# A dense 3x3 convolution of 192 channels on TensorE: 96 + 96 channels in 18 passes, or 128 + 64 channels in 15 passes with two image halves side by side

## The chip, the core and the metric

The kernel runs on one core of one Trainium2 chip. The time is device microseconds of that core for one execution of the whole kernel, and the median of several executions is given. TensorE is called PE below, the weight loads of TensorE PEld, VectorE DVE, ScalarE ACT, GpSimd POOL, and SyncE SP (its queue issues the transfers). All numbers are float32.

## The reference, cut to what matters

Four layers work on x of 16 images, 192 channels and 32 x 32 pixels, each with a residual and a group norm ahead of it. Only layer 0 is concerned here. After an mLSTM block over the 1024 pixels of an image (layer norm, projections, a scan that the kernel does in chunks of 128 pixels, an output projection) it has this end:

```python
y = x1 + x2                      # mLSTM block + silu(seq @ w_lin + b_lin)
y = conv_general_dilated(y, conv2_w, (1, 1), ((1, 1), (1, 1)), ("NCHW", "OIHW", "NCHW"))
y = y + conv2_b[None, :, None, None]
mu = y.mean((0, 2, 3)); var = y.var((0, 2, 3))        # over all 16 images
y = (y - mu) / sqrt(var + 1e-5) * bn_g + bn_b
x = x + where(y >= 0, y, 0.01 * y)
```

So 192 channels go to 192 channels with nine taps, 16 times 1024 pixels, and layer 1 can't begin before the mean and variance over all images are known.

## The kernel before, in words

layer0 goes through 128 chunks of 128 pixels, eight for an image, four for a unit (half an image, 512 pixels). The loop over g (layer0_step) does the work of one chunk: p = scores x decays on DVE (L680), num and state on PE (L694, L706, L729), the scores of the next chunk (L649), the normalisation (layer0_norm) and the output of the chunk before (layer0_output). Beside it run "side" tasks, each a generator with a start and a due time in steps: Side.tick lets each advance in proportion to the time gone by. The front of a unit (layer0_front: load of x, group norm and layer norm, w_up at L502, w_lin at L522, w_q and w_k at L540) has 2.7 steps, twice an image. The convolution of an image (layer0_conv2) has the time from 9.2 steps after the image's first chunk on, four parts of 1.9 steps each.

What an engine then does in which order is settled when the program is built: a scheduler goes through the instructions by priority and by when their operands should be there, and fixes one order for each engine. Each engine works off its own order strictly, and waits where an operand isn't there. [...]

layer0_down (L782 on) writes half of an image into ypad: 96 partitions, 2 halves of the channels, and the image of 32 x 32 with a frame of zeros, 34 x 34. There are two ypad tiles, for even and odd images. layer0_conv2 reads ypad directly, with shifted views for the nine taps. A part is 96 outputs of half an image (16 rows, 512 pixels): nine taps times two halves of the input channels make 18 matmuls of 96 rows, 96 columns and 512 pixels that add up in one PSUM tile, "conv", of which there is one. Four parts are 72 matmuls an image. In the trace each f32 matmul is two records. Then ACT adds the bias (L465), DVE takes the statistics (L466), and a transfer stores y to y0 in DRAM (L467). After the last chunk the four parts of the last image are done with nothing beside them, and batch_norm (L312 on) makes scale and shift from the statistics. Layer 1 (layer1_front) loads y0 again.

Other matmuls already put several outputs on different columns of TensorE: depthwise (L1094), in layers 2 and 3, gives three or four outputs of 32 channels, ps[32 * g : 32 * g + 32].

Of the kernel before, what the change touches and what calls it, by code (L numbers as in the profile page):

```python
# [10 lines left out]
F32 = mybir.dt.float32  # L11
# [7 lines left out]
C = 192  # L19
HP = 96  # L20
DI = 384
S = 1024
W = 32
# [73 lines left out]
def lay_out(a):  # L97

    p96, p128 = Pack(HP), Pack(128)
    for n in ("ln_w", "ln_b", "b_down", "b_lin", "conv2_b", "bn_g", "bn_b"):  # L100
        p96.vec("0" + n, a["L0_conv_" + n])
    for n in ("b_up", "conv_k", "conv_b", "skip", "mh_w", "mh_b"):
        p128.vec("0" + n, a["L0_conv_" + n])
    gates = np.zeros((128, 2), np.float32)
    gates[:NH, 0] = a["L0_conv_b_i"]
    gates[:NH, 1] = a["L0_conv_b_f"]
    p128.add("0gates", gates)
    for n in ("norm_w", "norm_b", "proj_b"):
        p96.vec("1" + n, a["L1_conv_" + n])
    p96.add("1skip_scale", np.broadcast_to(a["L1_conv_skip_scale"].reshape(1, 1), (HP, 1)))  # L110
    p128.add("1conv_r", taps(a["L1_conv_conv_w"].reshape(DI, 1, 4)))
    for n in ("conv_b", "A_log", "D"):
        p128.vec("1" + n, a["L1_conv_" + n])
    p96.add("2w_r", taps(a["L2_conv_w"].reshape(C, 3, 3)))
    for n in ("b", "gamma", "beta"):
        p96.vec("2" + n, a["L2_conv_" + n])
    for n in ("b_out", "dw_b", "bn_g", "bn_b", "bn_mean", "bn_var", "pw_b"):
        p96.vec("3" + n, a["L3_conv_" + n])
    p96.add("3dw_r", taps(a["L3_conv_dw_w"].reshape(C, 3, 3)))
    p96.vec("3r_w", a["L3_conv_r_w"].T)  # L120
    p96.add("3r_b", np.broadcast_to(a["L3_conv_r_b"].reshape(1, 2), (HP, 2)))
    p128.add("3conv_r", taps(a["L3_conv_conv_w"].reshape(DI, 4, 4)))
    for n in ("b_in", "conv_b", "ln_g", "ln_b"):
        p128.vec("3" + n, a["L3_conv_" + n])
    p128.vec("3Ds", a["L3_conv_Ds"].T)
    p128.vec("3A_log", a["L3_conv_A_log"].transpose(1, 0, 2))

    def in96(w):
        return w.reshape(2, HP, -1).transpose(1, 0, 2)

    def in128(w):
        return w.reshape(w.shape[0] // 128, 128, -1).transpose(1, 0, 2)

    def dt_rows(w, b):
        o = np.zeros((64, DI), np.float32)
        o[:RK], o[XD] = w.T, b
        return o

    def pair(f, *v):
        rows = [np.concatenate([f(*(x[k] for x in v)), f(*(x[k + 2] for x in v))]) for k in range(2)]  # L140
        return np.stack(rows, 1)[: 64 + XD + 1]

    def x_rows(w):
        return np.concatenate([w, np.zeros((64 - XD, DI), np.float32)])

    wif = np.zeros((3 * DI, 44), np.float32)
    wif[:, :NH] = a["L0_conv_w_i"]
    wif[:, 32 : 32 + NH] = a["L0_conv_w_f"]
    const, const0 = shape_constants()
    arrays = {  # L150
        "x": a["x"].reshape(-1, C, S),
        "p96": p96.array(),
        "p128": p128.array(),
        "const": const.array(),
        "const0": const0.array(),
        "w0_up": in96(a["L0_conv_w_up"]),
        "w0_q": in128(a["L0_conv_w_q"]),
        "w0_k": in128(a["L0_conv_w_k"]),
        "w0_qt": in128(a["L0_conv_w_q"].T),
        "w0_kt": in128(a["L0_conv_w_k"].T),  # L160
        "w0_if": in128(wif),
        "w0_down": in128(a["L0_conv_w_down"]),
        "w0_lin": in96(a["L0_conv_w_lin"]),
        "w0_conv2": in96(a["L0_conv_conv2_w"].transpose(1, 2, 3, 0).reshape(C, 9 * C)),
        "w1_in": in96(a["L1_conv_in_proj_w"].T),
        "w1_x": in128(x_rows(a["L1_conv_x_proj_w"])[: XD + 1].T),
        "w1_dt": dt_rows(a["L1_conv_dt_proj_w"], a["L1_conv_dt_proj_b"])[: XD + 1],
        "w1_out": in128(a["L1_conv_out_proj_w"].T),
        "w1_proj": in96(a["L1_conv_proj_w"].T),
        "w3_in": in96(a["L3_conv_W_in"]),  # L170
        "w3_x": in128(pair(x_rows, a["L3_conv_x_proj_w"]).transpose(2, 1, 0).reshape(DI, -1)),
        "w3_dt": pair(dt_rows, a["L3_conv_dt_proj_w"], a["L3_conv_dt_proj_b"]).reshape(-1, 2 * DI),
        "w3_out": in128(a["L3_conv_W_out"]),
        "w3_pw": in96(a["L3_conv_pw_w"].T),
    }
    arrays = {k: np.ascontiguousarray(v) for k, v in arrays.items()}
    return arrays, p96.at, p128.at, const.at, const0.at
# [74 lines left out]
class Program:  # L252
# [35 lines left out]
    def run(self):  # L288
        tc, nc = self.tc, self.nc
        with tc.tile_pool(name="const", bufs=1) as cp, tc.tile_pool(name="scratch", bufs=1, space=DRAM) as dp:  # L290
            self.p96 = self.load(cp, "p96", list(self.ins["p96"].shape))
            self.p128 = self.load(cp, "p128", list(self.ins["p128"].shape))
            self.const = self.load(cp, "const", list(self.ins["const"].shape))
            self.y0 = dp.tile([self.nb, HP, 2, S], F32, name="y0")
            self.x2 = dp.tile([self.nb, HP, 2, S], F32, name="x2")
            self.y2 = dp.tile([self.nb, HP, 2, S], F32, name="y2")
            self.x3 = dp.tile([self.nb, HP, 2, S], F32, name="x3d")
            self.x1 = dp.tile([self.nb, HP, 2, S], F32, name="x1d")
            self.xf1 = dp.tile([self.nb, HP, 2, S], F32, name="xf1d")
            self.sz3 = dp.tile([2, 2, 128, 3, 512], F32, name="sz3")  # L300
            self.bn0 = cp.tile([HP, 2, 2], F32, name="bn0")
            self.bn2 = cp.tile([HP, 2, 2], F32, name="bn2")
            self.layer0()
            self.layer12()
            self.layer3()
# [64 lines left out]
    def layer0(self):  # L370
        tc = self.tc
        with (
# [5 lines left out]
        ):  # L378
            self.layer0_weights(wp, bp, psum)
            self.stats = wp.tile([HP, 2, 2 * self.nb, 6], F32, name="stats")  # L380
            self.unit, self.image = {}, {}
            n = self.nb * S // 128
            side = Side()
            for i in range(1, self.nb * S // U):
                side.add("front", self.layer0_front(i, sp, bp, dp, psum), NCH * i - 3.9, NCH * i - 1.2)
            for b in range(self.nb - 1):
                for j in range(4):
                    at = 8 * b + 9.2 + 1.9 * j
                    side.add("conv", self.layer0_conv2(b, j, bp, psum), at, at + 1.9)
            finish(self.layer0_front(0, sp, bp, dp, psum))  # L390
            self.layer0_decays(self.unit[0], sp, psum)
            chunks = {0: Chunk(self.unit[0], 0, 0)}
# [3 lines left out]
                for j, _ in enumerate(self.layer0_step(g, n, chunks, sp, bp, psum)):  # L396
                    side.tick(g + j / 8)
            side.close()
            for u in range(4):
                finish(self.layer0_conv2(self.nb - 1, u, bp, psum))  # L400
            self.batch_norm(sp, "0bn_g", "0bn_b", self.bn0)

    def layer0_weights(self, wp, bp, psum):
# [8 lines left out]
        self.w_c2 = self.load(wp, "w0_conv2", [HP, 2, 9, C])  # L412

        self.b_up = wp.tile([128, 6], F32, name="b_up")
        ps = psum.tile([128, 512], F32, name="mm")
# [15 lines left out]
        for c in range(3):  # L431
# [8 lines left out]
        self.v1, self.ypad = [], []  # L440
        for i in range(2):
            v1 = wp.tile([128, NH, DH + 1], F32, name=f"v1{i}")
            nc.vector.memset(v1, 1.0)
            yp = wp.tile([HP, 2, W + 2, W + 2], F32, name=f"ypad{i}")
            nc.gpsimd.memset(yp, 0.0)
            self.v1.append(v1)
            self.ypad.append(yp)

    def layer0_conv2(self, b, part, bp, psum):

        nc = self.nc
        yp = self.ypad[b % 2]
        m, i = divmod(part, 2)
        ps = psum.tile([128, 512], F32, name="conv", bufs=1)
        for t in range(9):
            for k in range(2):
                r0 = 16 * i + t // 3
                nc.tensor.matmul(  # L458
                    ps[:HP], self.w_c2[:, k, t, m * HP : (m + 1) * HP],
                    yp[:, k, r0 : r0 + 16, t % 3 : t % 3 + W],  # L460
                    start=t + k == 0, stop=t + k == 9,
                )
            yield
        y = bp.tile([HP, 512], F32, name="y", bufs=1)
        nc.scalar.activation(y, ps[:HP], AF.Identity, bias=self.v96("0conv2_b", m))  # L465
        nc.vector.bn_stats(self.stats[:, m, 2 * b + i], y)  # L466
        nc.sync.dma_start(self.y0[b, :, m, i * 512 : (i + 1) * 512], y)  # L467

    def layer0_front(self, i, sp, bp, dp, psum):

# [311 lines left out]
    def layer0_down(self, unit, psum):  # L782

        nc = self.nc
        b, u = divmod(unit["i"], S // U)
        yp = self.ypad[b % 2]
        rows = U // W
        for m in range(2):
            ps = psum.tile([128, 512], F32, name="mm")
# [355 lines left out]
    def layer1_front(self, b, sp, bp, psum):  # L1145
# [5 lines left out]
        nc.sync.dma_start(xf, self.y0[b])  # L1151
        yield Wait(1)
        for m in range(2):
            for h in halves():
# [479 lines left out]
```

## Time and profile before

| what | us |
|---|---|
| median of 3 runs | 17707.09 |
| lowest, highest | 17689.62, 17722.61 |
| the profiled execution's own time | 17751.62 |
| its span, first to last instruction | 17749.8 |
| last eviction of the convolution (L465) starts | 4200.95 |

The page gives, for each engine, its busy time in the span; then the span in 40 equal slices of 444 us, where a digit is the busy share in tenths and PEclk is the clock that TensorE was granted, in tenths of full speed. Groups of instructions stand in rows: line, engine, operation, output and inputs, shape, number of records, then busy time and mean duration in ns, then the idle time of the engine ahead of them and what ended it. In answers by window the columns are the stretch, its length, then for each engine busy time and number of records, then the granted clock (1 is full), the DMA share and GB/s. A row of the timeline has the start, the length, engine, line, operation, and in brackets how long the engine had been idle and what ended that. Layer 0 fills the first nine and a half slices.

### The profile page before, as it was taken

Reading aid. Unit: us, or ns where it says so; the run is one execution under the profiler, and the core shown is the slowest. Engines: PE = TensorE matmul, PEld = TensorE weight load, DVE = VectorE, ACT = ScalarE, POOL = GpSimd, SP = SyncE. Lnnn points to the kernel's source line nnn. Section 1 sums busy time; section 2 is a strip of 40 time slices with the busy share of each in tenths; the row PEclk is TensorE's granted clock in tenths of the full one; section 3 lists DMA queues with packets and bytes.
Section 4 is the critical chain, followed back from the end, with each engine's and each line's share of the span. In section 5 each row is a group of like instructions: output and inputs, shape, how many; then the busy total and the mean of one; then the engine's idle time right before and its main releaser. Section 6 shows DMA issues by size and latency. Waiting matters only on the chain. (4 is left out here: it accounts for less than half of the span.)

```text
span 17749.8 us, 263742 instructions
## 1 busy us (share of the span) xinstructions
PE 16096.1 (91%) x99836; PEld 11228.6 (63%) x99836; DVE 13328.7 (75%) x14875; ACT 11899.2 (67%) x19653; POOL 11473.1 (65%) x5556
## 2 busy tenths in 40 slices
PE   8998898898998999988999999999999999999998
PEld 4444444444655555555777777777777777777777
DVE  4454444444777777766898888888888888888888
ACT  2222222223666666656888888888888888888888
POOL 3333333333555555545887888788878888888888
PEclk8898988898999999999999999999999999999999
DMA  1111111112343333333333333333323332333232
GB/s 43 32 31 32 32 31 30 33 30 70 107 116 114 116 118 117 115 102 105 97 108 94 94 99 107 92 96 100 107 85 95 107 105 85 99 106 99 90 98 67
DMA packets 877952, 1511.10 MB, mean 85 GB/s; under 512 B 80337, under 2 KB 311198, under 8 KB 865835
## 3 DMA queue, kind: packets, MB, share of 16 engines
q1 hardware_dynamic: 876682, 1494.22, 28.9%
q8 instruction: 791, 12.96, 0.3%
q14 instruction: 479, 3.92, 0.1%
HBM read 1264.99 MB, written 228.92 MB: 84 GB/s over the span
## 5 line engine op out<-in xcount | busy, mean ns | idle before, releaser
L940 POOL TENSOR_TENSOR h<-h,cb 128x1536 f32<-128x1536 f32 x2560 | 8875.0, 3470 | 1429.5 <-DVE h L933 883.9
L909 ACT ACTIVATE da<-dt,neg_a 128x512 f32<-128x512 f32 x7680 | 5266.5, 714 | 1737.1 <-DVE h L933 1668.3
L933 DVE TENSOR_TENSOR_SCAN h<-da,carry,xb 128x512 f32<-128x512 f32 x3840 | 4652.8, 1262 | 664.4 <-PE xb L920 599.4
L951 PE MATMUL y<-const,h 128*128 128x128 f32 x30720 | 4717.6, 276 | 129.2 <-DVE ysum L1391 54.1
L933 DVE TENSOR_TENSOR_SCAN h<-da,xb 128x512 f32<-128x512 f32 x3840 | 4440.5, 1202 | 387.5 <-PE xb L920 275.3
L917 PE MATMUL xb<-const,xbt 128*128 128x128 f32 x23040 | 4076.6, 282 | 419.3 <-DVE h L933 263.2
L889 ACT ACTIVATE xbt<-ut,bt 128x384 f32<-128x384 f32 x7680 | 4173.9, 603 | 247.3 <-PE xb L917 245.2
L917 PEld LDWEIGHTS xb<-const,xbt 128*128 128x128 f32 x23040 | 2761.4, 143 | 1807.6 <-issue 642.0
L951 PEld LDWEIGHTS y<-const,h 128*128 128x128 f32 x30720 | 3685.1, 143 | 322.4 <-issue 265.3
L920 PE MATMUL xb<-diag,ut 128*128 128x128 f32 x15360 | 3017.2, 279 | 0.0
L920 PEld LDWEIGHTS xb<-diag,ut 128*128 128x128 f32 x15360 | 2384.6, 195 | 62.6 <-issue 62.6
L458 PE MATMUL conv<-ypad,w_conv 96*96 96x512 f32 x2304 | 1258.7, 667 | 3.1 <-ACT y L465 3.1
L899 POOL TENSOR_TENSOR diag<-const,bt 128x512 f32<-128x512 f32 x640 | 681.3, 1065 | 549.6 <-PE xb L920 365.7
L939 POOL COPY carry<-h 128x3 f32<-128x3 f32 x1280 | 250.5, 196 | 1214.2 <-DVE h L933 964.7
L753 POOL TENSOR_TENSOR hs<-h,mhm 128x384 f32<-128x384 f32 x128 | 106.6, 833 | 1023.2 <-DVE den L758 894.5
L636 POOL TENSOR_TENSOR e<-e,const 128x1536 f32<-128x1536 f32 x128 | 444.3, 3471 | 436.5 <-DMA e<-row 380.1
L458 PEld LDWEIGHTS conv<-ypad,w_conv 96*96 96x96 f32 x2304 | 381.4, 181 | 451.2 <-issue 432.1
L839 PE MATMUL mm<-dbl,w_dt 45*128 45x512 f32 x960 | 534.6, 641 | 33.9 <-DVE v L1413 16.2
L638 ACT ACTIVATE e<-e 128x1536 f32<-128x1536 f32 x128 | 189.6, 1481 | 460.6 <-POOL e L637 415.0
L706 PEld LDWEIGHTS num<-v,p 128*128 128x128 f32 x3072 | 427.7, 216 | 78.3 <-issue 56.2
L1094 PE MATMUL mm<-rep,t_dw 96*32 96x512 f32 x2304 | 434.7, 614 | 22.6 <-DMA rep<-xr 16.3
L843 DVE SCALAR_TENSOR_TENSOR dt<-lnsq,mm 128x512 f32<-128x512 f32 x480 | 321.9, 671 | 172.0 <-ACT lnsq L842 172.0
(269 smaller groups left out, 17699.4 us busy)
## 6 DMA issues: line engine op xcount, KB each, us to landing
cb<-row SPq DMA_DIRECT2D x2560, 256.0 KB
rep<-xr SPq DMA_DIRECT2D x384, 331.0 KB
e<-row SPq DMA_DIRECT2D x128, 768.0 KB
rep<-xin SPq DMA_DIRECT2D x384, 256.0 KB
rep<-xr SPq DMA_DIRECT2D x384, 228.8 KB
x<-x SPq DMA_DIRECT2D x48, 768.0 KB
xr<-xin SPq DMA_DIRECT2D x48, 612.5 KB
xr<-xpad SPq DMA_DIRECT2D x32, 867.0 KB
```

The costliest lines, as they stand in the source:

```text
L458: nc.tensor.matmul(ps[:HP], self.w_c2[:, k, t, m * HP : (m + 1) * HP], yp[:, k, r0 : r0 + 16, t % 3 : t % 3 + W], start=t + k == 0, stop=t ...
L636: nc.gpsimd.tensor_tensor(e, e, self.k0("mask")[:, None, :].to_broadcast([128, NH, 128]), ADD)
L839: nc.tensor.matmul(ps, w_dt[:, t * 128 : (t + 1) * 128], dbl, start=True, stop=True)
L889: nc.scalar.activation(t[:, c], u.ut[:, c], AF.Copy, scale=u.bt[:, c, n : n + 1])
L899: nc.gpsimd.tensor_tensor(d, ident[:, None, :].to_broadcast([128, 4, 128]), u.bt[:, 3, n : n + 4][:, :, None].to_broadcast([128, 4, 128]), ...
L909: nc.scalar.activation(da[i, t], u.dt[:, t], AF.Exp, scale=u.neg_a(t, n))
L917: in_order(nc.tensor.transpose(xb[i, t][:, c * 128 : (c + 1) * 128], xbt[i][:, c, t * 128 : (t + 1) * 128], ident))
L920: in_order(nc.tensor.matmul(xb[i, t][:, 384:], u.ut[:, 3, t * 128 : (t + 1) * 128], u.diag[n // 4][:, n % 4], start=True, stop=True, skip_ ...
L933: nc.vector.tensor_tensor_scan(hv, dv, xv, 0.0 if first else u.carry_in[:, n, t : t + 1], MUL, ADD)
L940: nc.gpsimd.tensor_tensor(h[i], h[i], u.c.pop(n)[:, None, :].to_broadcast([128, 3, 512]), MUL)
L951: in_order(nc.tensor.matmul(u.y[:, j], h[i][:, t, c * 128 : (c + 1) * 128], ident, is_transpose=True, start=n == 0 and j % 4 == 0, stop=n ...
L1094: self.nc.tensor.matmul(ps[32 * g : 32 * g + 32], blocks[:, g * side + r], seen, start=r == 0, stop=r == side - 1, skip_group_check=True,)
```

## The change

The input channels are no longer split into 96 + 96 but into 128 + 64, and so are the outputs.

- After layer0_down has filled ypad for an image, layer0_spread writes it to DRAM (yrows) and reads it back in another layout: ya has channels 0 to 127 on 128 partitions; yb has channels 128 to 191 on partitions 0 to 63, and on partitions 64 to 127 the same channels moved by one pixel. These are four transfers on SP's queue, the second to fourth after the first has landed.
- With ya the nine taps take nine passes of 128 rows. With yb two neighbouring taps of the last 64 channels take one pass (three passes of 128 rows), and the third tap of each image row one of 64 rows (three passes). 15 passes in all, not 18.
- Parts 0 and 1 are outputs 0 to 127 for each half of the image: 15 matmuls each. Part 2 is outputs 128 to 191 for both halves: one PSUM tile, the upper half image on columns 0 to 63 and the lower on columns 64 to 127, 30 matmuls in 15 pairs. 60 matmuls an image in three parts of 2.4 steps each.
- There is one ypad, one ya and one yb, for all images. The weights are laid out anew on the host (128 x 15 x 192), y0 is stored by channel, and layer 1 reads it back with a rearranged view.
- The statistics stand by 128 + 64 channels; at the end three stores and a load bring them through DRAM into the old layout, ahead of both batch norms.

The diff, cut to its core:

```diff
             for b in range(self.nb - 1):
-                for j in range(4):
-                    at = 8 * b + 9.2 + 1.9 * j
-                    side.add("conv", self.layer0_conv2(b, j, bp, psum), at, at + 1.9)
+                side.add("spread", self.layer0_spread(b, wp, dp), 8 * b + 9, 8 * b + 9.1)
+                for j in range(3):
+                    at = 8 * b + 9.6 + 2.4 * j
+                    side.add("conv", self.layer0_conv2(b, j, bp, psum), at, at + 2.4)
...
-            for u in range(4):
-                finish(self.layer0_conv2(self.nb - 1, u, bp, psum))
+            finish(self.layer0_spread(self.nb - 1, wp, dp))
+            for j in range(3):
+                finish(self.layer0_conv2(self.nb - 1, j, bp, psum))
+
+            rows = dp.tile([C, self.nb, 2, 6], F32, name="stat_rows", bufs=1)
+            nc = self.nc
+            nc.sync.dma_start(rows[:128], self.stats_a)
+            for i in range(2):
+                nc.sync.dma_start(rows[128:, :, i], self.stats_b[64 * i : 64 * i + 64])
+            nc.sync.dma_start(
+                self.stats, rows.rearrange("(m p) b i s -> p m (b i) s", p=HP)
+            )
...
+    def layer0_spread(self, b, wp, dp):
+        nc = self.nc
+        n = (W + 2) ** 2
+        rows = dp.tile([2, HP, n], F32, name="yrows", bufs=2)
+        nc.sync.dma_start(rows.rearrange("m p t -> p m t"), self.ypad.rearrange("p m a b -> p m (a b)"))
+        rows = rows.rearrange("m p t -> (m p) t")
+        nc.sync.dma_start(self.ya.rearrange("p a b -> p (a b)"), rows[:128])
+        yb = self.yb.rearrange("p a b -> p (a b)")
+        nc.sync.dma_start(yb[:64], rows[128:])
+        nc.sync.dma_start(yb[64:, : n - 1], rows[128:, 1:])
+        yield
...
     def layer0_conv2(self, b, part, bp, psum):
         nc = self.nc
-        yp = self.ypad[b % 2]
-        m, i = divmod(part, 2)
         ps = psum.tile([128, 512], F32, name="conv", bufs=1)
-        for t in range(9):
-            for k in range(2):
-                r0 = 16 * i + t // 3
+        outs = [(ps, 0, 0, part)] if part < 2 else [(ps[64 * i : 64 * i + 64], 128, 128, i) for i in range(2)]
+        for t in range(15):
+            for o, _, c0, i in outs:
+                if t < 9:
+                    src, k, dy, dx = self.ya, 128, t // 3, t % 3
+                else:
+                    src, k, dy, dx = self.yb, 128 if t < 12 else 64, t % 3, 0 if t < 12 else 2
+                r0 = 16 * i + dy
                 nc.tensor.matmul(
-                    ps[:HP], self.w_c2[:, k, t, m * HP : (m + 1) * HP],
-                    yp[:, k, r0 : r0 + 16, t % 3 : t % 3 + W],
-                    start=t + k == 0, stop=t + k == 9,
+                    o, self.w_c2[:k, t, c0 : c0 + o.shape[0]], src[:k, r0 : r0 + 16, dx : dx + W],
+                    start=t == 0, stop=t == 14, skip_group_check=True,
                 )
             yield
```

More of the change, by code (lines that the diff above doesn't have):

```diff
@@ L99, in lay_out @@
     p96, p128 = Pack(HP), Pack(128)
-    for n in ("ln_w", "ln_b", "b_down", "b_lin", "conv2_b", "bn_g", "bn_b"):
+    for n in ("ln_w", "ln_b", "b_down", "b_lin", "bn_g", "bn_b"):
         p96.vec("0" + n, a["L0_conv_" + n])
@@ L103, in lay_out @@
         p128.vec("0" + n, a["L0_conv_" + n])
+    bias = np.asarray(a["L0_conv_conv2_b"], np.float32)
+    p128.add("0conv2_b", np.stack([bias[:128], np.tile(bias[128:], 2)], 1))
     gates = np.zeros((128, 2), np.float32)
@@ L144, in x_rows @@
         return np.concatenate([w, np.zeros((64 - XD, DI), np.float32)])
+    taps9 = np.asarray(a["L0_conv_conv2_w"], np.float32).transpose(1, 2, 3, 0)
+    rest = taps9[128:]
+    pairs = np.concatenate([rest[:, :, 0], rest[:, :, 1]])
+    single = np.concatenate([rest[:, :, 2], np.zeros_like(rest[:, :, 2])])
+    conv2 = np.concatenate([taps9[:128].reshape(128, 9, C), pairs, single], 1)
     wif = np.zeros((3 * DI, 44), np.float32)
@@ L163, in lay_out @@
         "w0_lin": in96(a["L0_conv_w_lin"]),
-        "w0_conv2": in96(a["L0_conv_conv2_w"].transpose(1, 2, 3, 0).reshape(C, 9 * C)),
+        "w0_conv2": conv2.reshape(128, 15 * C),
         "w1_in": in96(a["L1_conv_in_proj_w"].T),
@@ L293, in run @@
             self.const = self.load(cp, "const", list(self.ins["const"].shape))
-            self.y0 = dp.tile([self.nb, HP, 2, S], F32, name="y0")
+            self.y0 = dp.tile([self.nb, C, S], F32, name="y0")
             self.x2 = dp.tile([self.nb, HP, 2, S], F32, name="x2")
@@ L380, in layer0 @@
             self.stats = wp.tile([HP, 2, 2 * self.nb, 6], F32, name="stats")
+            self.stats_a = wp.tile([128, self.nb, 2, 6], F32, name="stats_a")
+            self.stats_b = wp.tile([128, self.nb, 6], F32, name="stats_b")
             self.unit, self.image = {}, {}
@@ L411, in layer0_weights @@
         self.w_down = self.load(wp, "w0_down", [128, 3, C])
-        self.w_c2 = self.load(wp, "w0_conv2", [HP, 2, 9, C])
+        self.w_c2 = wp.tile([128, 15, C], F32, name="w0_conv2")
+        nc.sync.dma_start(self.w_c2, self.ins["w0_conv2"].rearrange("p (t c) -> p t c", c=C))
         self.b_up = wp.tile([128, 6], F32, name="b_up")
@@ L439, in layer0_weights @@
             nc.vector.tensor_copy(self.w_g[:, c], ps[:, :44])
-        self.v1, self.ypad = [], []
+        self.v1 = []
         for i in range(2):
@@ L443, in layer0_weights @@
             nc.vector.memset(v1, 1.0)
-            yp = wp.tile([HP, 2, W + 2, W + 2], F32, name=f"ypad{i}")
-            nc.gpsimd.memset(yp, 0.0)
             self.v1.append(v1)
-            self.ypad.append(yp)
+        self.ypad = wp.tile([HP, 2, W + 2, W + 2], F32, name="ypad")
+        nc.gpsimd.memset(self.ypad, 0.0)
+        self.ya = wp.tile([128, W + 2, W + 2], F32, name="ya")
+        self.yb = wp.tile([128, W + 2, W + 2], F32, name="yb")
+    def layer0_spread(self, b, wp, dp):
[9 more added lines that the diff above has]
+        yield
@@ L458, in layer0_conv2 @@
                 nc.tensor.matmul(
-                    ps[:HP], self.w_c2[:, k, t, m * HP : (m + 1) * HP],
-                    yp[:, k, r0 : r0 + 16, t % 3 : t % 3 + W],
-                    start=t + k == 0, stop=t + k == 9,
+                    o, self.w_c2[:k, t, c0 : c0 + o.shape[0]], src[:k, r0 : r0 + 16, dx : dx + W],
+                    start=t == 0, stop=t == 14, skip_group_check=True,
                 )
             yield
-        y = bp.tile([HP, 512], F32, name="y", bufs=1)
-        nc.scalar.activation(y, ps[:HP], AF.Identity, bias=self.v96("0conv2_b", m))
@@ L466, in layer0_conv2 @@
-        nc.vector.bn_stats(self.stats[:, m, 2 * b + i], y)
-        nc.sync.dma_start(self.y0[b, :, m, i * 512 : (i + 1) * 512], y)
+        y = bp.tile([128, 512], F32, name="y", bufs=1)
+        nc.scalar.activation(y, ps, AF.Identity, bias=self.v128("0conv2_b", part // 2))
+        if part < 2:
+            nc.vector.bn_stats(self.stats_a[:, b, part], y)
+            nc.sync.dma_start(self.y0[b, :128, part * 512 : (part + 1) * 512], y)
+        else:
+            nc.vector.bn_stats(self.stats_b[:, b], y)
+            for i in range(2):
+                nc.sync.dma_start(self.y0[b, 128:, i * 512 : (i + 1) * 512], y[64 * i : 64 * i + 64])
@@ L785, in layer0_down @@
         b, u = divmod(unit["i"], S // U)
-        yp = self.ypad[b % 2]
+        yp = self.ypad
         rows = U // W
@@ L1150, in layer1_front @@
         xf = bp.tile([HP, 2, S], F32, name="xf", bufs=1)
-        nc.sync.dma_start(xf, self.y0[b])
+        nc.sync.dma_start(xf, self.y0[b].rearrange("(m p) t -> p m t", p=HP))
         yield Wait(1)
```

## The prediction, made before the changed kernel was run

> **What bounds the kernel now.** I read the page first: the convolution that changes (L458, filler work of layer 0) ends at 4200 us, and from there on the built programs of before and after have the same instructions in the same order on every engine (y0's reload apart). So only the first 4205 us can move, slices 0 to 9 of the 40.
>
> ```profile
> span 17749.8 us, 263742 instructions
> ...
> PE   8998898898998999988999999999999999999998
> ...
> PEclk8898988898999999999999999999999999999999
> ```
>
> TensorE (PE) is at eight or nine tenths there, no other engine above half, and the granted clock is the lowest of the run. But busy is not work. In the groups of instructions:
>
> ```profile
> L458 PE MATMUL conv<-ypad,w_conv 96*96 96x512 f32 x2304 | 1258.7, 667 | 3.1 <-ACT y L465 3.1
> L1094 PE MATMUL mm<-rep,t_dw 96*32 96x512 f32 x2304 | 434.7, 614 | 22.6 <-DMA rep<-xr 16.3 <-DVE dt L843 6.2
> ```
>
> Both have 2304 records of 512 elements and nearly the same mean, yet the second is busy for a third of the time: its three outputs lie on different columns (L1094 is the depthwise convolution of a later layer). The timeline gives the true rates:
>
> ```profile
> 4135.81 15.70 PE L458 MATMUL conv<-ypad,w_conv 96*96 96x512 f32 x36 [0.77 <-ACT y L465]
> ...
> 4698.08 2.78 PE L1094 MATMUL mm<-rep,t_dw 96*32 96x512 f32 x18
> ```
>
> 36 records in 15.70 us are 0.43 us each, as a matmul is two records: 0.86 us a matmul[...]. 18 records on three column strips in 2.78 us: six times 0.43 and a little.
>
> Then windows, cut where the first state product (L729) of a chunk starts. One image is eight chunks. Image 0 runs almost without convolution, image 2 with all of it (144 records):
>
> ```profile
> 135.10:371.90 236.80, 209.50 (x808) 124.50 (x807) 133.43 (x223) 69.85 (x104) 96.41 (x57) 0.73 0.13 31
> 371.90:608.90 237.00, 217.61 (x871) 113.70 (x870) 113.37 (x219) 67.67 (x99) 82.78 (x51) 0.89 0.12 33
> 608.90:863.70 254.80, 230.87 (x924) 117.12 (x923) 121.26 (x225) 70.33 (x104) 90.29 (x55) 0.89 0.13 31
> ```
>
> The convolution's 128 missing records are 55 us of PE at full clock, but image 0 is only 18 us shorter than image 2: its clock was 0.73, not 0.89. The same windows for steps of the image, with the convolution's records alone:
>
> ```profile
> 216.60:290.90 74.30, 0.00 (x0) 0.00 (x0) 0.00 (x0) 0.61 0.12 32
> 410.00:452.40 42.40, 6.11 (x12) 1.70 (x12) 0.66 (x1) 0.91 0.12 34
> 649.70:707.40 57.70, 19.20 (x34) 5.79 (x34) 0.68 (x1) 0.88 0.13 34
> 707.40:777.20 69.80, 25.79 (x40) 7.72 (x40) 0.68 (x1) 0.80 0.13 32
> ```
>
> Steps 1 and 2 (rows 2 and 3): 22 records fewer, 9.4 us, made them 15.3 us shorter. There PE is the bound. Steps 3 and 4 (rows 1 and 4): 40 records fewer made them 4.5 us longer, at clock 0.61. There the chain of a new image (group norm, layer norm, activations: the waits of L354 on ACT v, 65.9 us, and DVE x, 34.1 us) is the bound, and the convolution fills its holes and keeps the clock up.
>
> [...] at the ends of L1094's runs the next start comes some 0.09 us later than inside, and 0.09 us before them: I take 0.2 us for each run of column-tiled matmuls. [...] The nearest transfer here (xr<-xpad, 867 KB, the same 192 rows of 4624 B as the new one) has its first packet 0.85 us after issue, its last at 5.2 us in the median of the 16 of L1279 (9.8 for those of L1474, which share the engines with others).
>
> **Part by part.** *Matmuls.* Before 72 an image, 61.9 us. After 30 of 128 outputs (25.8 us) and 15 pairs of 64 outputs. Side by side a pair costs one matmul: 12.9 us. But the order of the built program splits pairs: the 480 half matmuls of 16 images stand in 224 runs, 90 of them single; rounding each run up to pairs gives 300 slots, not 240, so 16.1 us an image, and 14 runs x 0.2 = 2.8 us. Sum 44.7, saving 17.2 us an image at full clock.
>
> *Where it is saved.* Slots by step of the image, from both built programs (steps 0 to 7): before 4.5, 9.5, 8, 12, 8, 10, 8, 12; after 1.2, 5, 6.5, 5.5, 7, 6, 9, 9. Steps 0, 1, 2, 5, 6 lose 12.3 slots, 10.6 us, less 8 runs x 0.2: 8.9 us. I take it as whole, from rows 2 and 3. Steps 3, 4, 7 lose 10.5 slots, 9.0 us less 1.4: 7.6 us. Rows 1 and 4 speak for nothing or less; image 0 against image 2 passed 18 of 55 on: I take a third, 2.5 us. Less filler is a colder clock: I take 3 us more at half clock an image, 1.4 us. Sum 8.9 + 2.5 - 1.4 = 10.0 us an image. Bounds: all of it (17.2) and a loss (the fourth rival).
>
> *Spread* (new, four transfers on SP's queue an image: to DRAM and back). Its cover: after the last write of ypad, PE has w_lin, state, num, scores, the first three w_q and the state product queued ahead of the first new matmul. In the trace before these end 12.8 to 19 us after layer0_down's last matmul in that step, ypad being done 2.0 to 4.3 us after it. The spread: 5.2 us and about 0.5 for the landing, then ya's 128 rows some 4.5 us: 12 to 13 us after layer0_down. It just fits: I take 0; without cover, up to 10 us an image, as everything on PE queues behind that matmul. SP waits inside the spread, some 6 us; behind it stand the next image's x, a row store and the load of e, which is wanted a step (30 us) later: nothing. Single ypad: written again half an image later; nothing. Single ya, yb: the next spread waits for the last matmul of this image, which the built program has ahead of the next layer0_down: nothing.
>
> *Small edits.* An eviction and a statistic fewer an image (0.68 us on ACT, 0.69 on DVE) lie beside PE: nothing. y0's transfers stay four. A memset fewer on POOL, 144 KB more of weights at the start: within 1 us. [...] The reload of y0 in layer 1 in rows of 4 KB: nothing, 0.1 us at most each.
>
> *Tail.* Nothing hides it. Before, from ypad's last write (4132.4) to the last batch norm value (4206.4): 74 us. After: spread 12, three parts of 15 slots 3 x (12.9 + 1.0), about 3 for a cold start and modes, eviction and statistic 1.4, the statistics through DRAM (three stores, two of them with 24-byte pieces, and a load) 10 within 6 to 20, two batch norms 6: 74. So 0, within 10 either way.
>
> Sum: 15 images x 10.0 = 150 us. The profiled execution took 17751.6 (span 17749.8 and 1.8 around it): 17602. It lies 44.5 above the median of the three runs; the same 150 from 17707.1 gives 17557. A measurement of this kernel can tell about 0.2% (35 us) from no change.
>
> **Rivals.** (1) All passes on: PE-bound everywhere, 17.2 x 15 = 258, 17449. For it: PE at nine tenths, and rows 2 and 3, where more than the records' time was gained. Against: image 0. (2) The halves don't run side by side (it doesn't do what it says): 60 slots an image, 10.3 - 2.8 = 7.5 us; passed on as above (10.0 of 17.2) 4.4 us, 65 in all, 17642. Against: L1094. For: there the strips are 32 columns, no row here has 64. (3) The spread comes late: PE waits for ya up to 10 us in each image, which eats the 150: 17707, no change. For: the cover is short by my own sum; against: half clock lengthens the cover too. (4) Slower, by the clock: the filler gets thin where it held the clock up. Its price is half of each microsecond more at half clock. Time at half clock is 2 x (1 - clock) of a window: 56 us in image 2, 128 in image 0. It decides from 35 us more an image on (17.2 / 0.5), clock 0.82 in the steady images. With 42 more, clock 0.81: 21 lost, 17 won, 4 x 15 = 60 slower, 17767. For: image 0 and rows 1 and 4. Against: two thirds of the filler stay, in every step.
>
> **How the numbers follow.** Forecast (60 to 235 us gained): 0.58. Rival 1: 0.12. Rival 2: 0.08. Rival 3: 0.10. Rival 4: 0.12. Faster by over 0.2%: 0.58 + 0.12 + 0.08 = 0.78; within: 0.10; slower: 0.12. The range holds rivals 1 and 2, the forecast and half of rival 3: 17440 to 17710; about 0.18 is left out.
>
> **What would show it.** Pairs side by side: 30 records of the last image's third part in some 13 us and not 26, in the timeline. The pass-on: image windows of 245 us, from 255, and steps 1 and 2 shorter, 3 and 4 not. The clock: 0.88 to 0.9 in them; 0.82 speaks for rival 4, and that would make the prediction wrong, as would waits of conv on DMA ya of more than 15 us in all. Layers 1 to 3 must keep their length, 13545 us, within 20.

## The result, and the profile after

The changed kernel takes 17581.5 us (median of 4 runs, 17569.7 to 17603.6), the kernel before beside it on the same chip 17706.4 (4 runs): ratio 0.9925, interval 0.9914 to 0.9937, 125 us faster. The forecast was 17557 with a range of 17440 to 17710. The profiled execution of after took 17603.6 (span 17601.8); that of before 17751.6: 148 us less, for the 150 of the sum. Medians and profiles differ because before's profiled execution lay 45 us above its median and after's 22; all accounts below are between profiled executions.

The page of after, to be held against the lines of before:

```profile
span 17601.8 us, 263080 instructions
...
PE   8988898897988899878999999999999999999998
...
PEclk7888888888999999989999999999999999999999
...
L500 PE MATMUL conv<-ya,w_conv 128*64 128x512 f32 (+1 forms) x1152 | 578.6, 706 | 27.8 <-ACT y L506 21.3
```

In the first ten slices, which hold layer 0, PE is less busy in the third and the tenth, and the clock is a tenth lower in the first, third, fifth and ninth. The slices are 440 us long and not 444, so the digits behind them cut the later layers elsewhere; their length is given below. The convolution now stands in two groups; the one shown (the passes on ya) has 1152 records.

The timeline of after in the last image, where nothing else runs (start, length, engine, line, tile, count):

```profile
4006.28 9.99 PE L500 MATMUL conv<-ya,w_conv 128*128 128x512 f32 x18 [6.56 <-DMA ya<-yrows]
...
4036.51 7.95 PE L500 MATMUL conv<-ya,w_conv 128*64 128x512 f32 x36 [0.78 <-ACT y L506]
4044.28 5.47 PE L500 MATMUL conv<-yb,w_conv 128*64 128x512 f32 x24
```

The third part is 60 records, 30 matmuls, from 4036.51 to 4049.75: 13.2 us. The halves run side by side, as the prediction wanted to see. The bracket of the first line is the only wait of the convolution for the spread in the whole trace.

Windows of after, cut at the first state product (now L775) of chunks 0, 8, 16 and 24, as those shown of before:

```profile
123.40:359.80 236.40, 204.99 (x786) 122.97 (x785) 134.43 (x223) 68.86 (x104) 96.36 (x57) 0.72 0.13 31
359.80:602.10 242.30, 221.83 (x873) 114.91 (x872) 126.90 (x220) 68.79 (x102) 91.55 (x56) 0.85 0.17 41
602.10:838.40 236.30, 211.95 (x899) 108.46 (x898) 119.97 (x224) 69.48 (x103) 84.86 (x54) 0.90 0.18 43
```

Image 2 took 236.3 for before's 254.8, but image 1 took 5 us more. One image is a poor sample (the thirteen of after scatter by 5.9 us around their mean), so from here an image is the mean of the thirteen of chunks 16 to 120. They in one window, first before:

```profile
608.90:3930.20 3321.30, 2988.35 (x11988) 1525.68 (x11987) 1621.41 (x2925) 918.04 (x1352) 1173.73 (x715) 0.89 0.13 32
```

then after:

```profile
602.10:3811.20 3209.10, 2872.42 (x11675) 1466.12 (x11674) 1622.54 (x2912) 905.89 (x1339) 1176.19 (x714) 0.86 0.16 41
```

255.5 us an image became 246.8: 8.6 less before rounding. The clock fell from 0.89 to 0.86. The clock records of both traces hold only 1 and 0.5 (232 stretches at 0.5 in before, 266 in after), so twice what is missing from 1 is the share of time at half clock, 55 and 68 us an image.

Where the 148 us are, stretch by stretch: the start up to the first state product 11.7 (135.1 to 123.4); chunks 0 to 16, 4.9 lost; the thirteen images 112.2; chunk 120 to ypad's last write 15.6; from there to the last batch norm value 5.2 (74.0 to 68.8); layers 1 to 3, 8.1 (13543 to 13535).

### The profile page after: what moved, and what is told of

Its sections match the earlier page's. It is cut to its first block, busy times and chain, and to the rows that moved or that the text cites. A ratio compares the mean times of both kernels' runs of the same rounds, so it can differ in the third digit from the quotient of the medians.

```text
span 17601.8 us, 263080 instructions
## 1 busy us (share of the span) xinstructions
PE 15936.2 (91%) x99452; PEld 11143.2 (63%) x99452; DVE 13342.1 (76%) x14859; ACT 11884.1 (68%) x19637; POOL 11481.6 (65%) x5555
## 5 line engine op out<-in xcount | busy, mean ns | idle before, releaser
L500 PE MATMUL conv<-ya,w_conv 128*64 128x512 f32 (+1 forms) x1152 | 578.6, 706 | 27.8 <-ACT y L506 21.3
L371 PE MATMUL mm<-lnsq,const 96*96 96x512 f32 (+1 forms) x576 | 352.2, 697 | 143.5 <-ACT lnsq L370 118.1
L548 PE MATMUL mm<-xn,w_up 96*128 96x512 f32 x768 | 427.6, 693 | 45.3 <-DVE ypad L840 32.9
```

The lines of the kernel that those rows point to most:

```text
L500: nc.tensor.matmul(o, self.w_c2[:k, t, c0 : c0 + o.shape[0]], src[:k, r0 : r0 + 16, dx : dx + W], start=t == 0, stop=t == 14, skip_group_c ...
```

## Experiments

The theory after the result: an image is the sum of four things. They are the convolution's slots (a slot is the time of one matmul, 0.86 us at full clock: 0.43 us from record to record, with 96 rows in before and 128 in after; a pair of half matmuls side by side takes one; the six matmuls of 64 rows and 128 columns in after's image count as one each too, though alone between others they take 1.05 us at full clock), counted in the order of the instructions as in the prediction; half of the time at half clock; PE's waits; and a remainder that doesn't change. "Filler" is the convolution's matmuls between the others. The rivals: the change between half matmuls and the rest eats the gain; the shape of the matmuls sets the clock; or the place of the filler in PE's order matters, not its amount. The table has all twelve runs; each ratio is to executions of before on the same chip beside it. Image, half clock (from the trace's clock records) and PE's waits (the view of waits) are us an image over the thirteen; the remainder is image - 0.86 x slots - half clock / 2 - waits.

Each row's account is of one execution. That of before lies 45 us above its median and that of after 22 us, that of late 26 us below and that of nudge 44 us; 15 us are 1 us an image. So a difference of under some 3 us an image between two rows is no effect by itself.

| kernel | median us | ratio, interval | image | slots | half clock | waits | remainder |
|---|---|---|---|---|---|---|---|
| before | 17706 | 1 | 255.5 | 72 | 55.1 | 25.4 | 140.5 |
| after | 17581 | 0.9925, 0.9914-0.9937 | 246.8 | 49.2 | 68.1 | 25.8 | 144.7 |
| one_pass | 17340 | 0.9781, 0.9767-0.9796 | 231.1 | 4 | 106.1 | 31.9 | 142.7 |
| filler | 17656 | 0.9964, 0.9951-0.9977 | 248.1 | 74 | 36.5 | 20.3 | 145.9 |
| serial | 17608 | 0.9929, 0.9913-0.9946 | 246.8 | 60 | 58.8 | 21.1 | 144.7 |
| no_spread | 17572 | 0.9912, 0.9897-0.9927 | 247.1 | 49.2 | 67.9 | 26.2 | 144.7 |
| before_pad | 17675 | 0.9974, 0.9965-0.9983 | 252.0 | 72 | 47.0 | 26.0 | 140.5 |
| before48 | 17427 | 0.9836, 0.982-0.9852 | 237.9 | 48 | 63.0 | 23.8 | 141.3 |
| grouped | 17573 | 0.9921, 0.9903-0.9939 | 245.3 | 47 | 64.3 | 28.8 | 143.9 |
| late | 17510 | 0.9882, 0.9866-0.9898 | 238.3 | 50 | 58.3 | 18.0 | 148.1 |
| nudge | 17614 | 0.9934, 0.9922-0.9946 | 244.3 | 50.8 | 63.5 | 23.4 | 145.4 |
| late_grouped | 17587 | 0.9923, 0.9911-0.9936 | 246.3 | 48 | 73.8 | 22.7 | 145.4 |
| before_late | 17727 | 1.0002, 0.9994-1.001 | 255.1 | 72 | 65.1 | 20.1 | 140.5 |
| late_nudge | 17576 | 0.9918, 0.9905-0.9932 | 244.6 | 50.2 | 65.6 | 22.3 | 146.3 |

The remainder of the four kernels with the old convolution is 140.5 to 141.3, whatever else they change: the account holds there to 1 us. With the new one it is 142.7 to 148.1, so it holds less well: some 4.1 us more in after than in before, of which the prediction's price for the runs of half matmuls is 2.8. A wait at half clock is counted twice, so a row can be off by a few us; late is the worst.

### one_pass: how much is left to gain

```diff
-        for t in range(15):
+        for t in range(1):
```

> Leaves out 14 of the 15 passes of every part, so the convolution is one tap only: 4 slots of 0.86 us an image, not 49. My theory (filler that partly hides, and that holds the clock up): the image falls to about what image 0 of the kernel before had without convolution, 237 us, at clock 0.74, so 10 us an image less than the changed kernel, and 36 us less at the tail: about 17395 us, ratio to before 0.982. Rival (TensorE is the bound everywhere, each slot passed on whole): 39 us an image less, 580 in all, about 16965, ratio 0.958, at an unchanged clock.

Measured: ratio 0.9781, near the theory's 0.982 and far from the rival's 0.958, though the image fell to 231.1 and not to 237. 45 slots fewer than after are 38.9 us; the image became 15.7 shorter. Half clock rose by 38 us (19 us lost) and the waits by 6. The window of its thirteen images shows the clock at 0.77:

```profile
587.20:3591.30 3004.10, 2586.51 (x10219) 1524.75 (x10218) 1728.71 (x2912) 907.28 (x1339) 1192.72 (x716) 0.77 0.18 44
```

So even of nearly the whole convolution only two fifths of the slots' time can be had from here. The filler keeps the clock up, and half of what is removed is paid for in clock.

### filler: the slots of before put back

```diff
-        for t in range(15):
+        for t in [0] * 8 + list(range(15)):
```

> The changed kernel with the first pass of each part done nine times instead of once (the extra eight are overwritten): 74 slots an image, as many as the 72 of the kernel before. My theory: the steady image goes back to about 255 us and the clock to 0.89, with 20 us more at the tail: about 17725 us, ratio 1.001. Rival (slots passed on whole): 21 us an image over the changed kernel, 17581 + 320 + 20, about 17920, ratio 1.012. Second rival (the gain is not in the slots but in the new order or the buffers): it stays near 17600, ratio 0.994.

Measured: 74 slots, 17656, ratio 0.9964, which none of the three forecasts met. 25 slots more (21.3 us) lengthen the image by 1.3 us only, as half clock falls from 68.1 to 36.5 (15.8 us won) and the waits by 5.5:

```profile
605.60:3830.80 3225.20, 2959.97 (x12507) 1472.65 (x12506) 1555.48 (x2912) 907.44 (x1339) 1167.17 (x716) 0.93 0.16 41
```

PE executes 832 records more in the thirteen images than after, and they pass in 16 us more. Both runs show the same feedback from the two sides. Of after's 266 stretches at half clock all but ten last 3.4, 6.8, 10.2 or 13.7 us (114, 74, 45 and 23 of them); what starts and ends one is not seen in the traces.

But the theory had 255 us for this image, and it is 248.1. With about the same number of slots as before (74 and 72) the new kernel is 7.4 us an image shorter (some 5 by the medians), so the removed slots alone do not make the 8.6 us: most of the difference remains when they are put back. before_pad below takes up a part of it; the rest, in the order of the instructions or the hand-overs, stays open.

### serial: the halves one after the other

All fifteen taps of the upper half image, then all of the lower:

```diff
-        for t in range(15):
-            for o, _, c0, i in outs:
+        for o, _, c0, i in outs:
+            for t in range(15):
```

> The changed kernel with part 2 in another order: all 15 taps of the upper half image, then all 15 of the lower, so no two neighbours lie on different columns: 60 slots an image, not 49. My theory: 11 slots, 9.5 us at full clock, of which six tenths show: 6 us an image, 90 in all, and 13 at the tail: about 17685 us, ratio 0.999. Rival (halves never ran side by side within the image, only at the tail): 13 us more at the tail alone, 17595, ratio 0.994.

Measured: in the tail the same records take twice as long (timeline of serial):

```profile
4039.97 7.94 PE L500 MATMUL conv<-ya,w_conv 128*64 128x512 f32 x18 [0.78 <-ACT y L506]
4047.74 5.45 PE L500 MATMUL conv<-yb,w_conv 128*64 128x512 f32 x12
4053.13 7.94 PE L500 MATMUL conv<-ya,w_conv 128*64 128x512 f32 x18
```

18 records take 7.8 us up to the next start here; in after 36 do. The tail is 94.5 us for 68.8. Yet the steady image is the same, 246.8: the 10.8 slots more (9.3 us) come back as 9.3 us less at half clock (4.7) and 4.7 less of waits. The ratio, 0.9929, is nearer to the rival's 0.994 than to the theory's 0.999. Whether the halves run side by side within the images too, the timeline of after tells (image 8, at full clock):

```profile
2261.81 1.08 PE L500 MATMUL conv<-ya,w_conv 128*64 128x512 f32 x4
2262.82 0.55 PE L700 MATMUL mm<-const,k 128*128 128x128 f32 x3
...
2268.62 1.07 PE L500 MATMUL conv<-ya,w_conv 128*64 128x512 f32 x2
2269.62 0.55 PE L820 MATMUL mm<-const,hs 128*128 128x128 f32 x3
```

Two half matmuls (four records) take 1.01 us up to the next start, one (two records) takes 1.00; the medians over the thirteen images are the same. So they do run side by side, and the rival falls. serial's edit also moves the filler (16 slots in step 0, for 1.2 in after), so its unchanged image is not the price of the pairs alone.

### no_spread: the transfers taken out

The spread is done for the first image alone.

> The changed kernel with the four spread transfers done for image 0 only; later images convolve image 0's rows again. Takes away the transfers and what waits for them. My theory (the spread is hidden): nothing in the image, 7 us less at the tail where it isn't hidden: 17575 us, ratio 0.9925. Rival (TensorE, or SP's queue, waits for the spread in each image): 5 to 10 us an image, 75 to 150 less: 17430 to 17505, ratio 0.984 to 0.989.

```diff
+        if b:
+            return
         rows = dp.tile([2, HP, n], F32, name="yrows", bufs=2)
```

Measured: image 247.1 for 246.8, tail 61.8 for 68.8; ratio 0.9912, within after's interval. The spread is hidden in all images but the last, where it shows 7 us. The rival of the late spread is out.

### before_pad: the old matmuls on the full array

The 96x96 matmuls padded with zeros to 128x128, weights and ypad on 128 partitions.

```diff
-                    ps[:HP], self.w_c2[:, k, t, m * HP : (m + 1) * HP],
+                    ps, self.w_c2[:, k, t, m * 128 : (m + 1) * 128],
```

> The kernel before with its 72 matmuls widened with zeros from 96 rows and 96 columns to 128 and 128: same order, same number, same 0.43 us a record; the weights come on 128 partitions (2.4 MB, not 1.3). Open is why the run with 74 slots an image was 7.4 us an image quicker than the kernel before with 72, with 37 us at half clock in place of 55. Theory of the area (the clock follows how much of the array is in use): steady image 248 us, some 37 us of it at half clock, 110 us less in all, a few less at the start: ratio 0.993. Rival (order, buffers or hand-overs make those 7.4 us): image 255 us, half clock 55 us, ratio 0.999.

Measured: same slots, image 3.5 us shorter, 0.9974. The waits stay; half clock falls by 8.1 us, of which half is 4.1. So a wider matmul did go with a warmer clock, by about half of what I had expected: 3.5 of the 7.4 us between before and filler. It does not decide the clock alone: after has wider matmuls than before, but fewer slots, and a colder clock.

### before48: the slots of after in the kernel before

Twelve of eighteen matmuls a part.

```diff
-            for k in range(2):
+            for k in range(1 if t in (1, 2, 3, 5, 6, 7) else 2):
```

> The kernel before without 6 of the 18 passes of each part (taps 1, 2, 3, 5, 6, 7 of channels 96 to 191 left out): 48 slots an image of 96 rows and columns, in the old order, without spread and column tiles. Rival (the number of slots alone makes the gain): the image as in the changed kernel, 247 us, and 20 us less at the tail: ratio 0.991. Theory of the area: fewer narrow passes let the clock fall further, half clock over 75 us, image 251 to 254 us, ratio 0.995 to 0.998.

Measured: 0.9836, image 237.9; both forecasts missed, for the gain is twice what the rival had. 24 slots are 20.6 us, and 17.6 arrive: 4.0 go to the clock, 1.6 come from shorter waits, 0.7 is remainder. With nearly the same slots after is 8.9 us an image slower. By the table: slots 1.0, clock 2.6, waits 2.0, remainder 3.3. So after's gain is less than its slots are worth by three terms of like size, and not by one.

### grouped: fewer runs of half matmuls

The third part yields after five taps and not after each: 90 runs of half matmuls for 224.

```diff
-            yield
+            if part < 2 or t % 5 == 4:
+                yield 1 if part < 2 else 5
```

> The changed kernel with part 2 handed out in three pieces of five taps: 90 runs of column-tiled matmuls in place of 224, 47 slots an image. By my prediction's price (0.86 us a slot, 0.2 us a run): 2 slots and 9 runs less, 3.7 us an image at full clock, of which six tenths: 33 us less than the changed kernel, ratio 0.9905. Rival (slots in the image are nearly made up for by the clock): no difference, ratio 0.9925.

Measured: 0.9921, not to be told from after; but the interval (0.9903 to 0.9939) holds both forecasts, so the run does not decide between them. The price of a run can be read in after's trace itself, at full clock: the last start before a run of half matmuls comes 0.52 us ahead of it and not 0.43, and a run of one pair takes 1.01 us and not 0.86. That is 0.24 us a run, 3.4 us an image for 14 runs, most of the remainder's 4.1. The 8 runs fewer of grouped should then take 2.0 off; the image is 1.5 shorter and the remainder 0.8 lower, which is within the error of a row. So these changes take a part of the gain, but half of what the clock takes (6.5 us).

### late: the same work, due later

```diff
-                    at = 8 * b + 9.6 + 2.4 * j
-                    side.add("conv", self.layer0_conv2(b, j, bp, psum), at, at + 2.4)
+                    at, end = ((10.7, 12.4), (12.4, 14.6), (14.6, 16.8))[j]
+                    side.add("conv", self.layer0_conv2(b, j, bp, psum), 8 * b + at, 8 * b + end)
```

> The changed kernel with its three parts due from 10.7, 12.4 and 14.6 steps to 16.8, not from 9.6 on: 50 slots an image as before, but 7 of them moved from steps 1 and 2 to steps 0, 3 and 4. By the prediction's view (slots cost their whole time in steps 1 and 2 and a third in steps 3 and 4): 4 us less an image, 60 in all: ratio 0.989. Rival (it doesn't matter where they are): no difference, 0.9925. Third (the holes and the clock in steps 1 and 2 lack them): slower, above 0.994.

Measured: 17510, ratio 0.9882: 71 us faster than after by the medians, the fastest here of the kernels that compute everything. The forecast of the first theory (0.989) was met, but not by its mechanism: steps 1 and 2 together took 48.1 us for 48.2 with 5.5 slots fewer, and the gain is in steps 0, 4 and 6 (4.0, 3.0 and 2.3 us). Slots are nearly the same; half clock falls by 9.8 us and the waits by 7.8. The profiled execution is the fastest of its four and the warmest, so its image is some 1.6 us too good: the mean clocks of the four are 0.948, 0.943, 0.946 and 0.946, those of after's four 0.943, 0.946, 0.944 and 0.945, which leaves some 3 of the 9.8 us. The longest waits of PE in the thirteen images (us in all, times, longest), for after:

```profile
PE mm L820 <- DVE kt L701: 98.2, 26, 5.7
PE mm L371 <- ACT lnsq L370: 76.3, 13, 6.4
PE mm L568 <- DVE ypad L840: 30.2, 12, 4.2
```

and for late:

```profile
PE mm L820 <- DVE kt L701: 86.8, 36, 6.0
PE mm L548 <- DVE ypad L840: 25.1, 13, 2.1
PE mm L371 <- ACT lnsq L370: 20.8, 9, 4.6
```

L371, a layer norm's sum of squares, lost three quarters of its wait. The timeline of after, step 4 of image 8, shows the place:

```profile
2178.68 1.96 PE L363 MATMUL mm<-x,const 96*96 96x512 f32 x4
2180.57 0.93 PE L695 MATMUL s<-q,k 32*128 32x128 f32 x18
2187.64 2.02 PE L371 MATMUL mm<-lnsq,const 96*96 96x512 f32 x2 [6.15 <-ACT lnsq L370]
```

L363 makes the mean; from it DVE (xn, L365) and ACT make lnsq; L371 wants that. Between them PE has 0.9 us of score matmuls, and then stands, though further matmuls lie behind in its order: two score records start at 2189.60, straight behind L371, and a convolution matmul at 2190.32. What it stands for is DVE's order. DVE starts xn 5.6 us after L363's end, because other work lies ahead of it:

```profile
2179.75 3.09 DVE L804 TENSOR_SCALAR den<-den 128x12 f32<-128x12 f32 x1
...
2183.22 3.10 DVE L786 SCALAR_TENSOR_TENSOR state<-state,dec 128x132 f32<-128x132 f32 x3
2186.25 1.27 DVE L365 TENSOR_TENSOR xn<-x,mm 96x512 f32<-96x512 f32 x2
```

The same place in late:

```profile
2131.02 2.02 PE L363 MATMUL mm<-x,const 96*96 96x512 f32 x2 [1.14 <-DVE x L527]
2132.97 1.22 PE L695 MATMUL s<-q,k 32*128 32x128 f32 x10
2134.11 2.08 PE L500 MATMUL conv<-ya,w_conv 128*128 128x512 f32 x2
2135.98 1.92 PE L371 MATMUL mm<-lnsq,const 96*96 96x512 f32 x2
```

DVE starts xn at once here:

```profile
2133.07 1.28 DVE L365 TENSOR_TENSOR xn<-x,mm 96x512 f32<-96x512 f32 x2 [0.37 <-PE mm L363]
```

And a convolution matmul lies between, 2 us at half clock. So it does in serial, in the kernel before and in before48 (28.0, 30.6 and 18.5 us of this wait); not in grouped and filler (60.5 and 59.1). But the matmul between can cover only a part of the 6 us. From L363's end to L371's start it is 6.7 us on the mean of the thirteen images in after, 3.6 in late, and 2.2 in filler, which has no convolution matmul there either. So it is the work ahead in DVE's order that makes the wait.

### nudge: only that matmul put between

```diff
-                    at = 8 * b + 9.6 + 2.4 * j
+                    at = 8 * b + 9.8 + 2.4 * j
```

> All windows of the parts 0.2 of a step (some 6 us) later: 9.8 + 2.4 j in place of 9.6 + 2.4 j, nothing else. In the built order of the changed kernel the layer norm's matmul L371 of an image's first unit stands straight behind nine score matmuls (L695), with no convolution matmul between it and L363; here one stands there (five scores, one convolution matmul, L371), as in late, serial and the kernel before. Theory A (the gain of late came from that one wait: L371 on ACT lnsq 76.3 us in all, 13 times 5.9, against 20.8): the wait falls to under 25 us, the image by 4 to 5 us to 242, the total by some 65 us to 17515. Theory B (the gain of late came from how many slots stand in which step): a shift of 0.2 steps is a fifth of late's, some 1.7 us an image, 17555. Theory C (the wait only moves to the next instruction that needs the same chain): L371's wait falls, another rises, 17570 to 17590.

Measured: 0.9934, no gain by the medians (the image of its profiled execution is some 3 us too good). L371's wait fell to 18.7, but two new ones stand in its place:

```profile
PE mm L700 <- ACT q L590: 27.1, 6, 5.7
...
PE mm L706 <- ACT q L590: 24.7, 7, 4.1
...
PE mm L371 <- ACT lnsq L370: 18.7, 10, 4.1
```

27.1 and 24.7 in all are 4.0 us an image, all in step 1: five slots stand in step 0 now, for 1.2 in after, and q, whose matmuls (L586) are behind them in PE's order, is waited for. Theory A, that late gained by that one wait, has fallen; C, that the wait only moves, is what the runs show.

### late_grouped, before_late, late_nudge: is there a rule?

late_grouped is late and grouped together.

> Both edits at once: the windows of late and the third part in three pieces of five taps (89 runs of half matmuls for 247, 48 slots for 50). If grouped's 8 us and late's 71 us add: 17502, image 237. If grouped's gain in the image (1.5 us) came from the same wait that late takes away: 17510, as late. If pieces of ten half matmuls hold up what stands behind them (4.3 us at a time), slower than late, 17530.

Measured: 17587, 0.9923; late's gain is gone; of the three forecasts only the third (slower than late) had that, though less of it. The image is 8 us longer, all of it in step 7 (35.0 for 26.1 us), where 11 slots stand for 9 and 15.5 us are at half clock for 5.0. The wait of w_lin's matmul (L568) on ypad, gone in late, is back (33.2 us in all).

before_late has the four parts of before in late's windows.

```diff
-                    at = 8 * b + 9.2 + 1.9 * j
-                    side.add("conv", self.layer0_conv2(b, j, bp, psum), at, at + 1.9)
+                    at = 8 * b + 10.7 + 1.525 * j
+                    side.add("conv", self.layer0_conv2(b, j, bp, psum), at, at + 1.525)
```

> The kernel before with its four parts due from 10.7 to 16.8 (1.525 steps each) in place of 9.2 to 16.8. Its order already has a convolution matmul between the two layer norm matmuls. If a later filler is good in itself (theory B), some 71 us off: 17636. If late gained by the one wait that the changed kernel's order had made (theory A), nothing is gained here, and 72 slots in a shorter stretch fill steps 4 to 7 (12, 12, 10, 16 for 8, 10, 8, 12): 17700 to 17800.

Measured: 1.0002. The waits fell by 5.3 us, and half clock rose by 10.0. Late filler is not good in itself: with before's matmuls B falls.

late_nudge shifts late's windows by 0.2 of a step, to 10.9, 12.6, 14.8 and 17.0.

> The windows of late once more 0.2 of a step later: 10.9 to 12.6, 12.6 to 14.8, 14.8 to 17.0; nothing else. Slots by step (0 to 7) 5, 0, 4, 10, 6, 7.8, 8.2, 9.2 for late's 3, 0.5, 5.5, 9, 7, 7, 9, 9; a convolution matmul still stands between the two layer norm matmuls. If late's gain belongs to having the filler late (a region of orders), it stays: ratio 0.987 to 0.990, 17490 to 17540, image 237 to 240. If late is one good order among many, in which small shifts open and close waits (as nudge and late_grouped suggest), it falls back to the changed kernel's: 0.991 to 0.995, 17570 to 17620, image 244 to 247, with the time in step 0 or 1, where the slots are moved to.

Measured: 0.9918, some 65 us slower than late. Step 0 has 5 slots again, and nudge's waits are back:

```profile
PE mm L700 <- ACT q L590: 29.3, 6, 6.1
PE mm L706 <- ACT q L590: 26.9, 7, 4.5
```

late is one good order, in which neither wait is open, and a shift of 0.2 of a step already leaves it. That its profile is warmer than late_nudge's (58.3 for 65.6 us at half clock) is not shown to belong to the order: the mean clocks of all executions, 0.946 and 0.945, are as near as executions of one kernel are to each other.

## Why the prediction was right, step by step

The sum was 150 us; 148 were measured between the profiled executions and 125 between the medians. That it came so near is luck in part: two terms of the image were wrong, with opposite sign, and places that were put at nothing made up for the rest.

**Matmuls** (17.2 us saved at full clock): 22.8 slots by 0.86 are 19.6, less 4.1 of remainder: 15.5. Right in size (the terms by steps sum to 16.5, not 17.2, as they count half a slot more); 13.2 us for the pairs of a part in the tail, 12.9 and the price of its changes in the sum. That the slots alone make the gain is not shown: see filler.

**What is passed on** ("I take a third" in steps 3, 4 and 7): this step failed. By it 5.1 of the 16.5 us would have become waits; the waits grew by 0.4. Steps 0 to 7 went from 43.7, 33.4, 22.6, 24.0, 45.0, 31.4, 24.5, 31.0 to 41.8, 28.3, 19.9, 20.1, 51.7, 28.5, 29.4, 27.2. Steps 1 and 2 gained 7.8 together, as foreseen, but steps 3 and 7 gained 7.7, steps 4 and 6 lost 11.6. Only in step 4 did it go as this term had it, and more so: one slot fewer, 4.5 us more of waits and 7.7 more at half clock. In before48, where the order is the old one, step 3 gained 6.5. Image 0, from which I had drawn the third, was cold with hardly any filler, as one_pass is in all its images (0.77). And row 2 of the same windows already spoke against reading a share from one image: image 1 had 108 records of the convolution more than image 0 (46 us) and took the same 237 us.

**Clock** ("3 us more at half clock an image, 1.4 us"): failed. It was 13.0 us, 6.5 lost: nearly five times my term, and the chief reason why 15.5 became 8.6. The mean clocks of all executions on record, 0.950 for before and 0.9445 for after, give some 11 us for the 13. The two errors, 4.7 and 5.1, are of opposite sign; by that luck the 10.0 stood near 8.6. It was the mechanism of rival 4, at two fifths of the 35 us at which it would have decided.

**Images and the rest.** The chunks gained 123 (112.2 - 4.9 + 15.6) for 150. The 25 us that I had at nothing made that up: start, tail and layers 1 to 3.

**Start** ("within 1 us"): failed, 11.7 us better in these two profiles. The convolution's weights went from 96 rows of 13824 bytes to 128 of 11520, and the load became faster though larger. From 10 to 20 us the transfers ran at, for before,

```profile
10.00:20.00 10.00, 5.25 (x24) 5.19 (x24) 1.21 (x3) 0.00 (x0) 0.00 (x0) 1.00 1.05 253
```

and for after

```profile
10.00:20.00 10.00, 5.25 (x24) 5.19 (x24) 1.22 (x3) 0.00 (x0) 0.00 (x0) 1.00 1.04 378
```

GB/s (the last number). Behind that load is q's transposed weight, and the first matmul that wants it started at 31.8 us before and at 21.5 after. Over all profiles: 31.8, 28.6 and 22.6 where the weights lie on 96 partitions, 25.1 in before_pad and 20.0 to 23.7 (22.1 on the mean of ten) in the new form. The means differ by some 5 us (27.7 for the three), which is an estimate of what the change gives; the rest of the 11.7 is the scatter of the three, one of which lies among the new ones.

**Spread**: hidden, as forecast (no_spread). SP stood 4.2 us in each for the first transfer's landing (66.4 us in 16 times), for some 6. **Tail**: 5.2 better, within the 10. The spread took 8.5 us from its first issue to the first matmul, for 12; the first 18 records behind PE's wait for it took 9.8 us at clock 0.79, those of the next part 7.8 at 1.00; the statistics through DRAM 9.9 from the end of bn_stats to the aggregate, for 10. **Layers 1 to 3**: 13535, in the stated 13545 ± 20; no cause is shown for the 8 us.

**Rivals.** All passed on: no, by the clock. Not side by side: refuted by the tail and by the runs within the images. Late spread: refuted by no_spread. Slower by the clock: real, but not large enough.

## What to carry to other kernels

A filler matmul that is removed is not worth its own time: here a third of it (6.5 of 19.6 us) was lost again to half clock, and going the other way, 25 slots added to after cost 1.3 us for 21.3. It is no fixed rate either: in before48, 17.6 of 20.6 us arrived. Make the account of slots, half clock and waits from the trace before and after, on a mean of many images, and compare the clock over several executions before reading it from one. When the amount of filler changes, set its due times anew: late added 71 us to the 125 of the change. But try each order on the chip, since a shift of 0.2 of a step lost it.

## What the runs showed of the hardware

**Load by partitions.** In the weights' load a row of 13824 bytes took 1108 ns on 96 partitions, one of 11520 bytes 457 ns on 128. An estimate from these, with the rows shared evenly by the 16 engines that the page counts: 96 x 1108 / 16 = 6.6 us for 1.33 MB, and 3.7 us for 1.47 MB; 200 and 403 GB/s. The two other profiles with 96 partitions had 950 and 912 ns (before48, before_late), the nine others with 128 partitions and 11520 bytes 451 to 475. before_pad, with 2.36 MB on 128 partitions, also ran faster than before in the same window:

```profile
10.00:20.00 10.00, 5.25 (x24) 5.20 (x24) 1.21 (x3) 0.00 (x0) 0.00 (x0) 1.00 1.05 357
```

By the same estimate the three profiles with 96 partitions had 0.5 to 0.6 of the rate of after's 128. The number of partitions was not changed by itself: the rows became shorter in after and longer in before_pad (18432 bytes), and both loads were faster. Why is not shown.

**Width and clock.** The same number of matmuls in nearly the same order, each on 128x128 and not 96x96, had 47.0 us at half clock for 55.1 (before_pad); over all executions the mean clock was 0.954 (11) for 0.950 (14). It is shown for this pair of kernels only; what sets it is not seen in these runs.
